# Two bottleneck blocks on one core: tiles as runs of 392 pixels, one tile less in the Gram matrix, three rows of the last tile made early

## The chip, the core and the metric

One core of a Trainium2 chip runs the whole program. The metric is the time of one execution on the device in microseconds (us). The kernel before takes 1884.95 us, the median of three runs (1884.44 to 1885.69).

## What is computed

Two bottleneck blocks stand one behind the other. Input and output are 64 images of 1024 channels and 14×14 pixels in fp32, which makes 64·196 = 12544 pixels in all. One block of the reference, cut to what matters:

```python
out = relu(_bn(_conv(x, w1, b1, 1, 0), g1, be1))      # 1x1, 1024 -> 256
out = relu(_bn(_conv(out, w2, b2, 1, 1), g2, be2))    # 3x3,  256 -> 256
out = _bn(_conv(out, w3, b3, 1, 0), g3, be3)          # 1x1,  256 -> 1024
out = softplus(residual_scale)[0] * out
return relu(x + out)
```

`_bn` takes mean and variance over images and pixels. So the sums over all 12544 pixels of a convolution's result have to be known before the first of its values can be normalized.

## The kernel before

Everything of 256 channels (`y`) stays in SBUF as `y_all`, 128 partitions by two slots `s` by 12544 pixels. The 12544 pixels are cut into 32 tiles `t` of 392 pixels (two images). In `y_all` a group of 8 images lies row by row, 112 pixels to a row, so a tile of two images is 14 runs of 28 pixels; `two(t, s)` (L88) gives that view. Values of 1024 channels are 8 rows `o` of 128 channels ("output rows"), and `x_t` is a tile of them, 128 partitions by 8·392.

The change bears on the end of block two, from about 1500 us on. It goes in three stages.

**The Gram stage.** The mean and the mean square of the third convolution's result are not taken from that result, which is not made yet, but from `y`: the Gram matrix of `y`'s 256 channels, with a column of ones, and the weights give both. `gram` (L1321) walks over the pixels by blocks of 128 pixels, two at a time (`CH`), 98 blocks or 49 pairs. A block has to stand with its pixels on the partitions; VectorE (DVE) transposes it by `turn` (L1310) from a buffer `home`, into which DMAs and ScalarE (ACT) have moved a piece of `y`. Then TensorE (PE) makes four products per block (`gram_products`, L1292) that add up in the banks `ap`. The pieces are listed in `moved`, and the last piece is the first 1536 pixels. At the start of the stage, while no block is there yet, PE convolves the first `HELD` = 5 rows of tile 0, and ACT copies them to `z` some time later.

**The gap.** When the last block is in, `conv3_stats` (L1745) makes the sums `mv` from the Gram matrix by a chain of small DVE and PE steps, and `affine` (L2031) makes `scale` and `shift`. PE has little to do meanwhile; rows 5, 6 and 7 of tile 0 (`conv3`, L1240) are put there.

**The last stage.** `final` (L1849) walks over tiles 1 to 30 by pairs t = 1, 3, …, 29 and by q = 0 to 3 in each pair; one (t, q) is a unit of class `Conv3Pair`, which makes rows q and q + 4 of both tiles by seven products instead of eight. A product goes to a PSUM bank `cx`, `cy` or `cp`; DVE adds it to a row of `x` (L533), or ACT copies it to `cu` (L336), from where GpSimd (POOL) adds it (L556, L664). Then ACT applies shift and relu (also L336), DVE does the same for one row in four (L673), and SP's queue sends the rows out (L676). Two units overlap. In the rows below, x_29 and x_30 are the last pair. The rows of tile 0 are finished beside the first units. Behind the last unit `ending` (L1823) makes tile 31 plainly: per row four PE records (two matmuls, a slot each, in two passes), the residual on DVE (`residual`, L1802, the instruction at L1807), the relu on ACT, and a DMA per two rows (L1840), the last ones smaller.

Each engine works through its instructions in the order that the code is recorded in; the recorder fixes the order when the program is built. An instruction that waits holds back all that stands behind it on its engine.

## Time and profile before

| what | value |
|---|---|
| median of three runs | 1884.95 us |
| the profiled execution's own time | 1884.47 us |
| its span, first to last instruction | 1882.7 us |
| PE busy | 1867.1 us, 99% |
| DVE busy | 1573.0 us, 84% |
| ACT busy | 1105.0 us, 59% |
| POOL busy | 742.5 us, 39% |
| bytes moved by DMA | 459.17 MB, 244 GB/s in the mean |

The span is 1.8 us shorter than the execution's time. PE's granted clock is full all along. In rows of a timeline the first number is the start in us, the second the time in us, and what stands in brackets is how long the engine sat idle just before and which engine and line ended that. "PEld" is the loading of weights, which overlaps PE, and SPq is SP's queue. A busy time printed for a group of matmuls includes the overlap of one with the next, so the starts say better than the lengths how fast PE goes.

### The profile page before, as it was taken

What the parts mean: (1) busy time and instruction counts of PE and PEld (TensorE: products, weight loads), DVE (VectorE), ACT (ScalarE), POOL (GpSimd) and SP (SyncE); (2) the same over time, 40 slices, a digit from 0 to 9 for tenths busy, and PEclk for the clock granted to TensorE, in tenths of its full rate; (3) what the DMA queues carried; (4) which work ended last, traced back from release to release, by engine and by line L of the source; (5) the groups of instructions that cost most, each with busy time, mean ns of one, the idle gap of its engine ahead of it and who ended that gap; (6) DMA issues with size and microseconds to landing.
All of it is one profiled execution on the core that took longest, in us unless ns stands there. A gap on an engine that the chain in (4) does not pass through costs nothing. (4 is left out here: it accounts for less than half of the span.)

```text
span 1882.7 us, 28588 instructions
## 1 busy us (share of the span) xinstructions
PE 1867.1 (99%) x9752; PEld 1559.0 (83%) x9752; DVE 1573.0 (84%) x2496; ACT 1105.0 (59%) x2301; POOL 742.5 (39%) x762
## 2 busy tenths in 40 slices
PE   9999999999999999999999999999999999999999
PEld 5555557999997998899999999999999987555555
DVE  5787867999998776778878888799999987888886
ACT  2222214677777665555555555457777794666666
POOL 0111100121205656377677776301121051666665
PEclk9999999999999999999999999999999999999999
DMA  7777654798765556678788789559788466999997
GB/s 289 269 253 270 216 188 128 211 215 220 206 197 169 186 173 212 248 272 312 275 287 307 276 307 278 209 169 220 213 208 227 135 179 245 350 336 333 349 338 280
DMA packets 263329, 459.17 MB, mean 244 GB/s; under 512 B 59376, under 2 KB 229712, under 8 KB 250000
## 3 DMA queue, kind: packets, MB, share of 16 engines
q1 hardware_dynamic: 224928, 375.47, 59.7%
q0 software_dynamic: 31408, 29.30, 8.0%
q10 hardware_dynamic: 6848, 52.57, 6.9%
q8 instruction: 77, 1.26, 0.3%
q14 instruction: 68, 0.56, 0.1%
HBM read 289.44 MB, written 141.03 MB: 229 GB/s over the span
## 5 line engine op out<-in xcount | busy, mean ns | idle before, releaser
L161 PE MATMUL columns<-v,ub 128*128 128x224 f32 (+1 forms) x1536 | 302.9, 339 | 1.3 <-ACT columns L336 0.8
L336 ACT ACTIVATE x<-x,shift 128x392 f32<-128x392 f32 x453 | 260.4, 613 | 70.4 <-DVE x L533 31.4
L161 PEld LDWEIGHTS columns<-v,ub 128*128 128x128 f32 x1536 | 268.6, 188 | 7.8 <-ACT columns L336 1.5
L336 ACT ACTIVATE cu<-cy,scale 128x196 f32<-128x196 f32 (+1 forms) x360 | 175.6, 500 | 166.6 <-PE cy L161 156.6
L161 PE MATMUL ay<-at,ws 128*128 128x196 f32 (+1 forms) x760 | 191.5, 383 | 0.4 <-ACT au L336 0.2
L664 POOL TENSOR_TENSOR x<-x,cu 128x392 f32<-128x392 f32 x120 | 126.0, 1051 | 104.9 <-DVE x L533 103.6
L161 PEld LDWEIGHTS ay<-at,ws 128*128 128x128 f32 x760 | 135.0, 190 | 35.5 <-ACT au L336 0.5
L533 DVE SCALAR_TENSOR_TENSOR x<-cp,scale,x 128x196 f32<-128x196 f32 (+1 forms) x240 | 124.7, 519 | 45.4 <-PE cp L161 43.9
L336 ACT ACTIVATE au<-ay 128x196 f32<-128x196 f32 (+1 forms) x139 | 53.5, 385 | 169.6 <-PE ay L161 159.6
L161 PE MATMUL l<-diffs,ub 128*128 128x224 f32 (+1 forms) x768 | 149.7, 337 | 0.5 <-DVE diffs L802 0.3
L161 PE MATMUL m<-sums,ua 128*128 128x224 f32 (+1 forms) x752 | 146.0, 337 | 1.2 <-issue 0.6
L161 PEld LDWEIGHTS l<-diffs,ub 128*128 128x128 f32 x768 | 134.6, 190 | 1.7 <-DVE diffs L802 0.7
L161 PEld LDWEIGHTS m<-sums,ua 128*128 128x128 f32 x752 | 131.4, 189 | 2.6 <-issue 1.0
L1103 POOL DMA_DIRECT2D y<-f x24 | 32.1, 1636 | 257.0 <-DVE f L1002 257.0
L161 PE MATMUL cx<-y,w 128*128 128x196 f32 (+1 forms) x400 | 123.1, 394 | 0.0
L556 POOL TENSOR_TENSOR x<-x,cu 128x196 f32<-128x196 f32 (+1 forms) x120 | 104.5, 871 | 45.8 <-ACT cu L336 28.7
L161 PE MATMUL cy<-y,w 128*128 128x196 f32 (+1 forms) x376 | 116.9, 399 | 1.8 <-ACT y L336 0.9
L336 ACT ACTIVATE y<-y,shift,scale 128x320 f32<-128x320 f32 (+9 forms) x107 | 110.7, 1061 | 7.1 <-DVE shift L2075 6.4
L561 POOL TENSOR_TENSOR x<-x,cu 128x392 f32<-128x392 f32 x60 | 80.3, 1339 | 85.1 <-DVE x L533 82.2
L208 POOL DMA_DIRECT2D u<-y x48 | 26.0, 543 | 211.1 <-ACT y L336 210.4
L1924 POOL TENSOR_SCALAR y<-y,scale 128x392 f32<-128x392 f32 x57 | 92.3, 1620 | 28.5 <-DVE scale L2268 28.5
L962 ACT ACTIVATE columns<-m 128x448 f32<-128x448 f32 (+1 forms) x144 | 70.9, 492 | 55.4 <-PE m L161 48.5
(315 smaller groups left out, 4508.2 us busy)
## 6 DMA issues: line engine op xcount, KB each, us to landing
ub<-u SPq DMA_DIRECT2D x92, 768.0 KB, 5.6
x<-in_x SPq DMA_DIRECT2D x35, 1568.0 KB, 8.5
x<-mid SPq DMA_DIRECT2D x32, 1568.0 KB, 7.7
out<-x SPq DMA_DIRECT2D x123, 392.0 KB, 6.7
mid<-x ACTq DMA_DIRECT2D x30, 1568.0 KB, 9.2
x<-in_x SPq DMA_DIRECT2D x108, 392.0 KB, 7.7
ua<-u SPq DMA_DIRECT2D x92, 256.0 KB, 3.2
z<-kept SPq DMA_DIRECT2D x60, 392.0 KB, 2.9
```

Source lines behind the costliest of these rows:

```text
L161: tc.keep_in_program_order(nc.tensor.matmul(*args, **kw))
L208: nc.gpsimd.dma_start(out=us[b][i][:, s, o], in_=u)
L336: tc.keep_in_program_order(nc.scalar.activation(*args, **kw))
L533: run(nc.vector.scalar_tensor_tensor(v, bank, self.scale[:, o : o + 1], v, ALU.mult, ALU.add))
L556: run(nc.gpsimd.tensor_add(self.part(1, 1), self.part(1, 1), u3))
L561: run(nc.gpsimd.tensor_add(v, v, self.u12))
L664: nc.gpsimd.tensor_add(v, v, self.u12[:, i * self.n : (i + 1) * self.n])
L962: copy(v, m, AF.Copy)
L1103: nc.gpsimd.dma_start(out=out_rows[3][:, o], in_=fa[:, o, :full], accum_op=ALU.add)
L1924: run(nc.gpsimd.tensor_scalar(z, z, scale[:, o : o + 1], None, ALU.mult))
```

## The change

Four things are changed.

1. `two(t, s)` is one run of 392 pixels (three and a half rows of 112 pixels of a group of images) and no longer 14 runs of 28. The host orders `x` and the result accordingly. All views with `h l` in them go.
2. Tile 0 is left out of the Gram matrix: the last piece of `moved` is (384, 1536) and no longer (0, 1536), `GRAM_TILES` is 48, and of the 98 blocks 95 remain, the last pair with one block alone. The 8 pixels of tile 0 that the piece still has are set to zero by a POOL memset (`leave_out`). Tile 0's part of the sums comes from its own eight rows: `save(o)` copies a row to `z` on ACT with a running sum (`accum_out`) and squares it in place with another, which gives `own`; DVE scales `own`, and `conv3_stats` adds it where it copied before.
3. For this, rows 5, 6 and 7 of tile 0 are convolved inside the last Gram piece and no longer in the gap.
4. The gap gets rows 0, 1 and 2 (`ENDED` = 3) of tile 31 in their place. ACT copies them to `held`. Their residual and relu are done in `final`, one beside each of the first three units of the last pair, and `ending` convolves rows 3 to 7 only.

The diff, cut to these:

```diff
+ENDED = 3
+GRAM_TILES = -(-(NPX - PX // P * P) // (CH * P))
...
     def two(t, s):
-        j = t % (GI // G)
-        return y_grp[:, s, t // (GI // G), :, j * G * W : (j + 1) * G * W]
+        return y_all[:, s, t * PX : (t + 1) * PX]
...
-        turned, moved = pieces[0], [*pieces[1:], (0, begin)]
+        whole = PX // P * P
+        turned, moved = pieces[0], [*pieces[1:], (whole, begin)]
...
+        def leave_out(k):
+            x, a, run = home(k)
+            nc.gpsimd.memset(x[:32, :, :, : PX - a], 0.0)
+
+        def save(o):
+            act(z[:, o], made[o], AF.Identity, accum_out=own[:, 0, o : o + 1])
+            act(made[o], made[o], AF.Square, accum_out=own[:, 1, o : o + 1])
...
-                    if k == len(moved) - 2 and i < len(made):
-                        act(z[:, i], made[i], AF.Copy)
+                    if k == len(moved) - 2 and i < HELD:
+                        save(i)
+                    if k == len(moved) - 1 and i < CS - HELD:
+                        o = HELD + i
+                        made.append(conv3(psum, 0, o, w3, ("cx", "cy")[i % 2]))
+                        save(o)
+            nc.vector.tensor_scalar(own, own, 1.0 / NPX, None, ALU.mult)
...
-        nc.vector.tensor_copy(mv[:, :, 0], sums[0][:, :, 0])
-        nc.vector.tensor_copy(mv[:, :, 1], sums[1][:, :, 0])
+        for i, ps in enumerate(sums):
+            if own is None:
+                nc.vector.tensor_copy(mv[:, :, i], ps[:, :, 0])
+            else:
+                nc.vector.tensor_add(mv[:, :, i], ps[:, :, 0], own[:, i])
...
+                if o >= ENDED:
+                    ps = psum.tile(PX // parts)
+                    for s in range(MS):
+                        matmul(ps, w3[:, s, o, :], two(T - 1, s)[:, here], start=s == 0, stop=s == MS - 1)
+                    residual(xt, o, ps, aff, here)()
...
                     while len(units) > 2:
                         units.pop(0).go_out()
+                    if t == T - 3 and q < ENDED:
+                        residual(xs[T - 1], q, held[:, q], aff)()
...
-                        made = [*(z[:, o] for o in range(HELD)), conv3(psum, 0, HELD, w3, "cx")]
+                        made = [conv3(psum, T - 1, 0, w3, "cx")]
+                        act(held[:, 0], made[0], AF.Copy)
...
-                    made += [conv3(psum, 0, HELD + 1 + i, w3, tag) for i, tag in enumerate(("cx", "ax"))]
+                    made += [conv3(psum, T - 1, 1 + i, w3, tag) for i, tag in enumerate(("cx", "ax"))]
                 aff = affine(mv3, pb, G3, BE3, conv_bias=B3)
+                if b == 1:
+                    for o in range(1, ENDED):
+                        act(held[:, o], made[o], AF.Copy)
```

Since the changed file is longer, some lines have new numbers after it: the matmul is L167 (before L161), ACT's helper L342 (L336), the residual L1816 (L1807), DVE's sums L536 (L533) and L676 (L673).

Three places show how the instructions move; the numbers behind the names are those of buffers. The first is PE's order at the end of the Gram stage. `ap<-zt` are the four products of a block, in three lines of which the first stands for two, and `cx<-y,w` and `cy<-y,w` are a plain row of the third convolution. After the change, from the second block of a pair on, with four and a half pairs of blocks still to come behind the first convolution:

```order
L167 MATMUL ap<-zt_11486 64x193 x2
L167 MATMUL ap<-zt_11486 64x129
L167 MATMUL ap<-zt_11486 64x130
L167 MATMUL cx<-y,w_1_11445 128x392 x2
L167 MATMUL ap<-zt_11487 64x193 x2
L167 MATMUL ap<-zt_11487 64x129
L167 MATMUL ap<-zt_11487 64x130
L167 MATMUL ap<-zt_11487 64x193 x2
L167 MATMUL ap<-zt_11487 64x129
L167 MATMUL ap<-zt_11487 64x130
L167 MATMUL cy<-y,w_1_11445 128x392 x2
```

Before, no convolution stands between the blocks: lines of `ap<-zt` follow one another up to the gap. Now rows 5 (`cx`), 6 (`cy`, the last line shown) and 7 (`cx`, one pair of blocks later) of tile 0 stand there.

The second place is DVE's order in the last pair. `x_29<-cx` and the like add a bank to a row of the pair. After the change:

```order
L536 SCALAR_TENSOR_TENSOR x_30_13851<-cp,scale,x_30_13851 128x392
L676 TENSOR_SCALAR x_27_13725<-x_27_13725,shift 128x392
L536 SCALAR_TENSOR_TENSOR x_30_13851<-cp,scale,x_30_13851 128x392
L536 SCALAR_TENSOR_TENSOR x_29_13849<-cy,scale,x_29_13849 128x392
L1816 SCALAR_TENSOR_TENSOR x_31_13973<-held,scale,x_31_13973 128x392 x3
L536 SCALAR_TENSOR_TENSOR x_29_13849<-cx,scale,x_29_13849 128x392
L536 SCALAR_TENSOR_TENSOR x_30_13851<-cp,scale,x_30_13851 128x392
L676 TENSOR_SCALAR x_27_13725<-x_27_13725,shift 128x392
```

Before, `x_29<-cy` and the `x_29<-cx` that is shown below it follow one another. Now the three residuals of tile 31 stand between them, all three in one place, where the pair's first two units overlap.

The third place is ACT's order there. `cu<-cy` copies a bank, and `x<-x,shift` is a relu. Before the change:

```order
L336 ACTIVATE x_28_13717<-x_28_13717,shift 128x392
L336 ACTIVATE x_27_13715<-x_27_13715,shift 128x392
L336 ACTIVATE x_28_13717<-x_28_13717,shift 128x392
L336 ACTIVATE cu_14051<-cy,scale 128x392
L336 ACTIVATE cu_14057<-cy,scale 128x392 x2
L336 ACTIVATE x_30_13841<-x_30_13841,shift 128x392
L336 ACTIVATE x_29_13839<-x_29_13839,shift 128x392
L336 ACTIVATE x_30_13841<-x_30_13841,shift 128x392
```

And after it:

```order
L342 ACTIVATE x_28_13727<-x_28_13727,shift 128x392
L342 ACTIVATE x_27_13725<-x_27_13725,shift 128x392
L342 ACTIVATE x_28_13727<-x_28_13727,shift 128x392
L342 ACTIVATE cu_14061<-cy,scale 128x392
L342 ACTIVATE x_31_13973<-x_31_13973,shift 128x392
L342 ACTIVATE cu_14069<-cy,scale 128x392 x2
L342 ACTIVATE x_30_13851<-x_30_13851,shift 128x392
L342 ACTIVATE x_29_13849<-x_29_13849,shift 128x392
L342 ACTIVATE x_30_13851<-x_30_13851,shift 128x392
```

The first relu of tile 31 stands between two copies: behind the last copy of unit q = 0 and ahead of the two copies of unit q = 1. The second and the third stand at the same place one and two units later.

More of the change, by code (lines that the diff above doesn't have):

```diff
@@ L1445, in pairs @@
             for k, (a, e) in enumerate(moved):
-                for i in range((e - a) // px):
-                    yield by_vector(k, i)
+                blocks = (e - a) // P
+                for i in range(-(-blocks // CH)):
+                    yield by_vector(k, i * CH, min(CH, blocks - i * CH))
                     if k + 2 < len(moved) and i in (1, 3):
@@ L1461, in gram @@
             if before is not None:
-                for c in range(CH):
-                    first, last = k == 1 and c == 0, k == total and c == CH - 1
+                n = before.shape[1]
+                for c in range(n):
+                    first, last = k == 1 and c == 0, k == total and c == n - 1
                     gram_products(upper, lower, before[:, c], first, last)
@@ L1565, in blocks @@
         def blocks(t):
-            return [[two(t, s)[:, i * H // 2 : (i + 1) * H // 2] for i in range(2)] for s in range(MS)]
+            return [[half_of(t, s, i) for i in range(2)] for s in range(MS)]
         n = PX // 2
```

100 lines of the change are left out of this document (42 added, 58 removed).

## The prediction

> **What bounds the kernel now.** I read the page's busy times first, then PE's waits, then the chain of waits from the Gram stage on, and last the timeline of the three places that the change touches.
>
> ```profile
> PE 1867.1 (99%) x9752; PEld 1559.0 (83%) x9752; DVE 1573.0 (84%) x2496; ACT 1105.0 (59%) x2301; POOL 742.5 (39%) x762
> ```
>
> PE is busy for 1867.1 of 1882.7 us: nothing but PE work taken away, or a new wait of PE's, moves the time much before the last few microseconds. The waits that PE has in the last stage are small:
>
> ```profile
> PE cy L161 <- ACT cu L336: 0.8, 4, 0.2
> ```
>
> All four waits for ACT's copies come to 0.8 us. So ACT's copies are in time now, and an edit that holds one back by more than its slack shows at once. The chain of waits has these rows at the end of the Gram stage:
>
> ```profile
> 1533.81 39.94 PE ap L161 x576
> 1573.75 1.51 PE cx L161 x4
> ```
>
> PE makes block after block without a pause: 576 records, at eight records a block (four products in two passes) 72 blocks, in 39.94 us, which is 0.555 us per block.
>
> **The change, part by part.**
>
> *Blocks left out.* Three of 98 blocks go, and PE is the limit there: 3 · 0.555 = **−1.66 us**. The zeroed pixels are one POOL memset, before the piece is transposed and on an engine that is idle there.
>
> *Rows moved.* The chain's rows of the ending:
>
> ```profile
> 1869.75 1.32 PE cx L161 x4
> 1871.06 1.32 PE cy L161 x4
> ...
> 1879.01 0.43 DVE x L1807
> ...
> 1879.47 0.46 ACT x L336
> ```
>
> A plain row costs PE 1871.06 − 1869.75 = 1.31 to 1.32 us. Three leave the ending (−3.95) and three more stand in the Gram stage (+3.95), where PE is the limit as well; the gap holds three rows as before, of another tile. On PE this is 0 in sum. The last stage starts 3.95 − 1.66 = 2.29 us later and its end is to come 3.95 us sooner after it.
>
> *ACT's saves.* Each of the eight rows of tile 0 costs ACT a copy and a square instead of a copy for five of them.
>
> ```profile
> L336 ACT ACTIVATE z<-cx 128x392 f32<-128x392 f32 x2 | 1.0, 505 | 0.0
> ```
>
> That is about 2 · 0.51 = 1.0 us per row, which the running sums may lengthen; no row shows those, so I bound it by 1.0 (they are free) and 2.0 us (they double it). The cover is ACT's and DVE's idle time at the end of the stage:
>
> ```profile
> 1573.86 1.56 DVE L1752 TENSOR_TENSOR g<-ap,by 64x65 f32<-64x65 f32 x5 [5.31 <-PE ap L161]
> ...
> 1574.94 0.20 ACT L1763 ACTIVATE g<-g 64x1 f32<-64x1 f32 x1 [12.60 <-DVE g L1752]
> ```
>
> ACT stood idle for 12.6 us before the gap and DVE for 5.3. The five early saves lengthen ACT's work by some 2.6 us. Row 7 leaves PE with five blocks to come, 5 · 0.555 = 2.8 us, so its save ends in front of the gap. `own`'s scaling on DVE waits for it, and then an add takes the place of a copy of the same few columns. I count all this as 0. If the saves took 2 us a row, the last would end about a microsecond after the last block, and the chain in the gap, on which PE waits, would be late by that: 0 to 1 us, and I take 0 by the row of 505 ns.
>
> *The residuals of tile 31.* They leave the ending, where PE was the limit, and stand in the last pair between instructions on which PE depends. In the order of ACT, the relu of row 0 now precedes the copies of the second unit, and in DVE's order its residual stands behind `x_29<-cy`. The rows of before at that place:
>
> ```profile
> 1853.06 1.20 ACT L336 ACTIVATE cu<-cy,scale 128x392 f32<-128x392 f32 x2
> ...
> 1854.78 0.82 PE L161 MATMUL cy<-ct,ws 128*128 128x392 f32 x2
> 1854.99 0.63 DVE L533 SCALAR_TENSOR_TENSOR x<-cy,scale,x 128x392 f32<-128x392 f32 x1
> 1855.03 1.01 POOL L664 TENSOR_TENSOR x<-x,cu 128x392 f32<-128x392 f32 x1 [0.32 <-DVE x L533]
> ...
> 1855.64 0.59 ACT L336 ACTIVATE cu<-cy,scale 128x392 f32<-128x392 f32 x1 [1.39 <-PE cy L161]
> ```
>
> The two copies of 1853.06 are the last of unit 0 and the first of unit 1; the second frees the bank that PE's product at 1854.78 writes. It ended at 1854.26, half a microsecond ahead. Now the relu stands between the two, and waits for a residual that DVE cannot start before `x_29<-cy` is through, at about 1855.55. Then POOL's sum runs until 1856.04. What that does to a DVE instruction with two operands in SBUF, as the residual of `held` is, shows one pair earlier:
>
> ```profile
> 1845.82 1.02 POOL L664 TENSOR_TENSOR x<-x,cu 128x392 f32<-128x392 f32 x1 [0.32 <-DVE x L533]
> ...
> 1846.43 0.83 DVE L497 TENSOR_TENSOR ct<-ct,y 128x392 f32<-128x392 f32 x1
> ```
>
> L497 ended at 1847.26, which is 0.42 us after POOL's end. Alone, a residual from SBUF takes 2.77 / 5 = 0.55 us:
>
> ```profile
> 1588.57 2.77 DVE L1807 SCALAR_TENSOR_TENSOR x<-z,scale,x 128x392 f32<-128x392 f32 x5
> ```
>
> So the residual ends at 1856.04 + 0.42 = 1856.46, the relu takes 0.55, the copy 0.59, and PE's product starts at about 1857.65 instead of 1854.78: **+2.87 us**. If POOL did not hold DVE up, the residual would end at 1855.55 + 0.55 = 1856.10, and the wait would be 2.5. The Trainium skill ("SBUF — State Buffer", section "Who interferes with whom") says that only the port pair which VectorE and GpSimd share is contended, "and it's an exclusive lock"; by this the residual is to stand still until POOL is done, as the row of L497 does, and the sum holds the 0.37 us more. The second and third relu stand at the same place one and two units later. Their residuals directly follow the first on DVE, are long done, and cost ACT 0.55 us each where the copy had 0.5 us to spare: +0.05 each, **+0.1 us**. DVE's next sum, `x_29<-cx`, comes 1.3 us later, which the wait of 2.87 us covers. The bounds of this part are 0, if x_31's row is ready before it is due in a way that I don't see, and what the second rival says.
>
> *The tail.* With 3.95 us less PE work, the last writes have less time.
>
> ```profile
> 1871.00:1877.00 6.00, 6.00 (x20) 3.50 (x19) 3.73 (x7) 3.28 (x6) 0.00 (x0) 1.00 1.02 383
> 1871.00:1882.00 11.00, 7.97 (x29) 4.89 (x27) 5.20 (x10) 5.33 (x10) 0.00 (x0) 1.00 0.78 291
> ```
>
> From 1871 on the DMA engines' mean busy share is 1.02 at 383 GB/s: they are full. 11 us at 291 GB/s are 3.20 MB. Rows 0 and 1 of tile 31 (0.39 MB) now go earlier, so 2.81 MB are left, 7.3 us at 383 GB/s, through at 1878.3 on the clock of before. The last issue and its landing:
>
> ```profile
> L1840 ACTq DMA_DIRECT2D out<-x x1: 344/344/344, 1880.0 to 1880.0; - x1
> ...
> DMA to landing us min/median/max: 1.7/2.1/4.0
> ```
>
> 1880.0 + 1.7 = 1881.7 was the last landing; by PE's chain it would be 1881.7 − 3.95 = 1877.75. The bytes are through at 1878.3, and I add 0.4 us for completion, since before the writes of the last 98 KB took 1.7 us from issue, of which the bytes are 0.3 and the rest spreads over issue and completion. 1878.7 against 1877.75 is **+1.0 us**, bounds 0 (rows 0 and 1 and one pair's rows go out earlier than I think) and 1.5 (the whole backlog plus a landing of 2.1).
>
> *Contiguous runs.* Whether `y` is read by runs of 28 or by 392 in one piece, the rows of the last stage show no difference:
>
> ```profile
> L161 PE MATMUL cy<-ct,w 128*128 128x392 f32 x117 | 48.2, 493 | 0.0
> L161 PE MATMUL cx<-y,w 128*128 128x392 f32 x116 | 47.7, 493 | 0.0
> L161 PE MATMUL cy<-y,w 128*128 128x392 f32 x116 | 47.7, 492 | 0.0
> ```
>
> `ct` is contiguous and `y` strided: 493, 493, 492 ns. I take 0.
>
> **Sum.** −1.66 + 2.87 + 0.1 + 1.0 = +2.3 us. The profiled execution took 1884.47 us (a span of 1882.7 and 1.8 around it) and would take 1886.8; the median of the runs is 0.5 above it, so on the runs I predict **1887.2 us**. A difference of 0.2%, 3.8 us, is about what a measurement of this kernel can tell from no change.
>
> **Rivals.**
>
> *The wait isn't there.* If the first residual is done in time (a record that the recorder puts elsewhere in time than I read, or slack on ACT that I missed), the gain of the blocks stays, and the tail takes between 0 and 1.0 of it: 1884.95 − 1.66 = 1883.3 to 1884.3. For it speaks that ACT is busy for 59% only; against it, that an engine's order is fixed and DVE's `x_29<-cy` cannot run earlier than the product it reads. Chance 0.22.
>
> *Tile 31 comes late: slower.* The first residual needs x_31, which nobody needed before the ending.
>
> ```profile
> L111 SPq DMA_DIRECT2D x<-mid x1: 325/325/325, 1847.1 to 1847.1; - x1
> ...
> DMA to landing us min/median/max: 7.7/7.7/7.7
> ```
>
> It was issued at 1847.1 and landed 7.7 us later, at 1854.8, only 1.2 us before POOL lets DVE go (1856.04). The loads of this pool from 1780 us on spread further:
>
> ```profile
> DMA to landing us min/median/max: 6.9/7.7/11.5
> ```
>
> With 11.5 us it lands at 1858.6, the residual ends at 1859.15 and not 1856.46, and everything behind is 2.7 us later still: +5.0, **1889.9 us**. The point from which it counts is a landing of 8.9 us; from 10.4 us on the whole is slower by more than 0.2%. For it speaks that the load shares the DMA engines with pair 27's writes; against it, that the change adds no transfer there and that 7.7 is also the median. Chance 0.16, of which 0.12 lies beyond 10.4 us.
>
> *Contiguous reads are faster.* The page has two groups of matmuls that read `y` as it lies:
>
> ```profile
> L161 PE MATMUL cx<-y,w 128*128 128x196 f32 (+1 forms) x400 | 123.1, 394 | 0.0
> ...
> L161 PE MATMUL cy<-y,w 128*128 128x196 f32 (+1 forms) x376 | 116.9, 399 | 1.8 <-ACT y L336 0.9
> ```
>
> These are 776 records; 8 ns off each would be 6.2 us and the time 1884.95 + 2.3 − 6.2 = 1881.0. The three rows above speak against it, with 1 ns between them. The Trainium skill ("Advanced Engine Details and Errata", section "PSUM Cachelines") has the rule that "Any non-contiguous AP significantly slows down matmuls"; the trace does not agree as far as it bears on the operand that is read, with 493 and 493 ns. Chance 0.05.
>
> **Chances.** Forecast 0.50, no wait 0.22, late tile 0.16, faster matmuls 0.05, and 0.07 for what I have not seen, of either sign. Forecast and first rival both lie within 0.2%. That makes 0.07 for faster, 0.77 for the same and 0.16 for slower. The range goes from the first rival's lower end to the second one's time: 1883.2 to 1890.0; the forecast's own terms (wait 2.5 to 2.9, tail 0 to 1.5, saves 0 to 1) reach from 1885.9 to 1888.7.
>
> **What would show it.** In the changed kernel's profile: the products `ap` end 1.66 us sooner but for three rows of 1.32 us among them; the gap keeps its length (if not, the saves are to blame); matmuls that read `y` stay at 492 to 494 ns; PE waits once for ACT's copy in the last pair, for 2.5 to 2.9 us, and ACT before it for DVE's residual (no such wait: first rival; a DVE wait for x_31's load: second); and the DMA engines are full from the last unit to the end, with a last landing about 2.7 us after the last matmul's relu. The forecast is wrong if PE's busy time falls by more than 2 us, or if the wait lies elsewhere.

## The result, and the profile after

The changed kernel takes 1890.66 us, the median of nine runs (1890.16 to 1891.72), against 1884.97 us for the kernel before on the same chip (nine runs, 1884.44 to 1886.55): a ratio of 1.0028, interval 1.0019 to 1.0037. It is slower by 5.7 us where +2.3 had been forecast, and lies just outside the range. The profiled execution took 1890.67 us with a span of 1888.9, which is 6.2 us more than before.

PE's busy time on the page of the changed kernel hardly differs from 1867.1:

```profile
PE 1867.8 (99%) x9728; PEld 1555.5 (82%) x9728; DVE 1573.1 (83%) x2494; ACT 1111.2 (59%) x2329; POOL 742.1 (39%) x763
```

So the time is in waits and in places where PE starts less often while it counts as busy. PE's waits in the changed kernel:

```profile
PE cy L167 <- ACT cu L342: 3.6, 5, 2.7
...
PE ap L167 <- DVE zt L1309: 0.9, 2, 0.6
```

The wait of 2.7 us is the one that the forecast named. The second row is PE waiting for DVE's transposes in the Gram stage, 0.2 us before. By PE's starts the 6.2 us divide as follows (us, from the timelines of the two profiled executions):

| stretch | before | after | difference | forecast |
|---|---|---|---|---|
| start of the first Gram product | 1518.14 | 1519.29 | +1.15 | 0 |
| Gram stage, first product to the row in the gap | 55.55 | 59.48 | +3.93 | +2.29 |
| gap, that row to the second row in it | 10.74 | 10.66 | −0.08 | 0 |
| the 120 records of PE from there on (first units of the last stage) | 40.87 | 41.57 | +0.70 | 0 |
| wait in the last pair | – | 2.87 | +2.87 | +2.97 |
| three rows of the ending | 3.95 | – | −3.95 | −3.95 |
| end of the last relu to end of span | 2.77 | 4.30 | +1.53 | +1.0 |

The first line lies ahead of all that runs differently; over the 14 profiles of this study (one execution each) that start lies between 1518.14 and 1520.00, and before is the earliest of them, so I count it as scatter.

**The Gram stage.** PE's rows of the changed kernel, from the long run of blocks to the gap:

```profile
1529.46 32.03 PE L167 MATMUL ap<-zt 128*64 128x193 f32 x464 [0.32 <-DVE zt L1309]
...
1562.11 6.80 PE L167 MATMUL ap<-zt 128*64 128x193 f32 x96 [0.62 <-DVE zt L1309]
...
1568.84 1.58 PE L167 MATMUL cx<-y,w 128*128 128x392 f32 x4
...
1570.36 1.32 PE L167 MATMUL ap<-zt 128*64 128x193 f32 x16
...
1571.60 1.58 PE L167 MATMUL cy<-y,w 128*128 128x392 f32 x4
...
1573.12 1.32 PE L167 MATMUL ap<-zt 128*64 128x193 f32 x16
...
1574.37 1.58 PE L167 MATMUL cx<-y,w 128*128 128x392 f32 x4
...
1575.88 2.96 PE L167 MATMUL ap<-zt 128*64 128x193 f32 x40
...
1578.78 1.58 PE L167 MATMUL cx<-y,w 128*128 128x392 f32 x4
```

The 39.94 us without a pause are broken by two waits for transposes, 0.32 + 0.62 = 0.94 us. A row among the blocks takes 1570.36 − 1568.84 = 1.52 us (then 1.52 and 1.51), not 1.32 as in the ending, and the pair of blocks behind it 1571.60 − 1570.36 = 1.24 us, where two blocks take 1.11. So each inserted row costs 0.20 us more in the row itself and 0.13 in the blocks behind it, some 0.33 us for going over from one kind of product to the other and back.

DVE is what PE waits for. The windows of the last full 15 us of transposing (PE, PEld, DVE, ACT, POOL busy, then clock and DMA), of the kernel before:

```profile
1550.00:1565.00 15.00, 15.00 (x220) 14.39 (x218) 15.00 (x29) 12.12 (x18) 5.50 (x10) 1.00 0.74 217
```

and of the changed kernel:

```profile
1550.00:1565.00 15.00, 14.38 (x210) 13.88 (x208) 14.74 (x26) 14.74 (x31) 6.79 (x19) 1.00 0.66 174
```

Before, PE *and* DVE were busy for 15.00 of 15 us. The forecast took PE for the one limit and made nothing of DVE's column here. DVE's rows say more about the two waits:

```profile
1528.70 1.30 DVE L1309 STREAM_TRANSPOSE zt<-home 128x512 f32<-128x512 f32 x2 [1.56 <-ACT y L342]
...
1552.69 1.30 DVE L1309 STREAM_TRANSPOSE zt<-home 128x512 f32<-128x512 f32 x2 [0.26 <-DVE zt L1309]
...
1561.36 1.29 DVE L1309 STREAM_TRANSPOSE zt<-home 128x512 f32<-128x512 f32 x2
```

Ahead of the first wait DVE itself had stood idle for 1.56 us, until ACT had a piece of `y` ready. From 1552.69 on DVE has no pause up to the transposes at 1561.36, for which PE waits the second time: there DVE's own work sets the pace. The 96 records behind that wait are the twelve blocks of the piece before the last, so neither the memset of the left-out pixels nor the landing of the last piece can have caused it.

**The saves**, on ACT in the changed kernel:

```profile
1570.46 0.50 ACT L342 ACTIVATE z<-cx 128x392 f32<-128x392 f32 x1 [5.03 <-PE cx L167]
1570.86 0.20 ACT L342 ACTIVATION_READ_ACCUMULATOR z<-cx 128x1 f32 x1
1570.95 0.49 ACT L342 ACTIVATE cx<-cx 128x392 f32<-128x392 f32 x1
1571.36 0.19 ACT L342 ACTIVATION_READ_ACCUMULATOR cx<-cx 128x1 f32 x1
```

Each running sum is an instruction of its own of 0.2 us. A row takes 1571.55 − 1570.46 = 1.09 us, and the last is done at 1577.08, 1.7 us before the gap: they cost nothing, as the gap's length says too.

**The last pair**, by all engines in the changed kernel:

```profile
1860.69 1.01 POOL L667 TENSOR_TENSOR x<-x,cu 128x392 f32<-128x392 f32 x1 [0.32 <-DVE x L536]
1861.18 2.02 DVE L1816 SCALAR_TENSOR_TENSOR x<-held,scale,x 128x392 f32<-128x392 f32 x3
1862.16 0.62 ACT L342 ACTIVATE x<-x,shift 128x392 f32<-128x392 f32 x1 [2.88 <-DVE x L1816]
1862.68 0.57 ACT L342 ACTIVATE cu<-cy,scale 128x392 f32<-128x392 f32 x1
...
1863.31 0.93 PE L167 MATMUL cy<-ct,ws 128*128 128x392 f32 x2 [2.71 <-ACT cu L342]
```

The residual waits behind POOL, the relu behind the residual (ACT idle for 2.88 us), the copy behind the relu, and PE's product behind the copy.

**The tail**, by windows of the changed kernel (columns as above):

```profile
1880.00:1884.00 4.00, 3.65 (x16) 2.37 (x14) 2.85 (x6) 2.75 (x5) 0.00 (x0) 1.00 1.02 373
1884.00:1888.00 4.00, 0.00 (x0) 0.00 (x0) 0.11 (x1) 0.46 (x1) 0.00 (x0) 0.73 0.80 292
```

The DMA engines are full at 1.02 while the last rows are made, and PE is done more than three microseconds before they are. In windows of 1 us from 1884 on they move 379, 394, 340, 53 and 0 GB/s: full almost to 1887, and then nothing for most of the last 1.9 us of the span.

**The first units of the last stage** hold 0.70 us that I had not looked at. Before, DVE's sum of two SBUF operands beside POOL's two sums:

```profile
1602.64 2.40 POOL L664 TENSOR_TENSOR x<-x,cu 128x392 f32<-128x392 f32 x2
...
1603.59 0.57 DVE L497 TENSOR_TENSOR ct<-ct,y 128x392 f32<-128x392 f32 x1
```

and the same three instructions in the changed kernel:

```profile
1607.65 1.98 POOL L667 TENSOR_TENSOR x<-x,cu 128x392 f32<-128x392 f32 x2
...
1608.61 1.45 DVE L502 TENSOR_TENSOR ct<-ct,y 128x392 f32<-128x392 f32 x1
```

DVE comes just as POOL goes from its first sum to its second. Before, DVE took 0.57 us, and POOL's two sums took 2.40; now POOL's take 1.98, and DVE takes 1.45. The Trainium skill ("SBUF — State Buffer", section "Who interferes with whom") has this as an exclusive lock that goes to whoever issues first, the other standing still; the lengths in the two traces agree, with 0.57 against 1.45 us. Who comes first cannot be read from the starts: in all 14 profiles DVE's is recorded 0.02 us ahead of POOL's second sum. In four of them (before, e1, e2, e5) DVE's instruction takes 0.57 us and PE's 120 records take 40.85 to 40.88; in the other ten it takes 1.45 and they take 41.56 to 41.63. As e2 and e5 have the change in them, this is not a cost of the change as such.

### The profile page after: what moved, and what is told of

Its sections match the earlier page's. It is cut to its first block, busy times and chain, and to the rows that moved or that the text cites. A ratio compares the mean times of both kernels' runs of the same rounds, so it can differ in the third digit from the quotient of the medians.

```text
span 1888.9 us, 28626 instructions
## 1 busy us (share of the span) xinstructions
PE 1867.8 (99%) x9728; PEld 1555.5 (82%) x9728; DVE 1573.1 (83%) x2494; ACT 1111.2 (59%) x2329; POOL 742.1 (39%) x763
## 5 line engine op out<-in xcount | busy, mean ns | idle before, releaser
L167 PE MATMUL columns<-v,ub 128*128 128x224 f32 (+1 forms) x1536 | 303.5, 339 | 1.4 <-ACT columns L342 0.8
L342 ACT ACTIVATE x<-x,shift 128x392 f32<-128x392 f32 x453 | 260.3, 613 | 71.7 <-DVE x L536 31.4
L167 PEld LDWEIGHTS columns<-v,ub 128*128 128x128 f32 x1536 | 268.6, 188 | 8.4 <-ACT columns L342 1.5
L342 ACT ACTIVATE cu<-cy,scale 128x196 f32<-128x196 f32 (+1 forms) x360 | 175.5, 499 | 163.0 <-PE cy L167 155.5
L167 PE MATMUL ay<-at,ws 128*128 128x196 f32 (+1 forms) x760 | 191.6, 383 | 0.4 <-ACT au L342 0.2
L167 PEld LDWEIGHTS ay<-at,ws 128*128 128x128 f32 x760 | 134.8, 190 | 35.7 <-issue 0.9
L536 DVE SCALAR_TENSOR_TENSOR x<-cp,scale,x 128x196 f32<-128x196 f32 (+1 forms) x240 | 124.4, 518 | 45.6 <-PE cp L167 44.2
L342 ACT ACTIVATE au<-ay 128x196 f32<-128x196 f32 (+1 forms) x139 | 53.5, 385 | 169.8 <-PE ay L167 159.8
L167 PE MATMUL l<-diffs,ub 128*128 128x224 f32 (+1 forms) x768 | 149.7, 337 | 0.4 <-DVE diffs L803 0.3
L167 PE MATMUL m<-sums,ua 128*128 128x224 f32 (+1 forms) x752 | 146.0, 336 | 1.2 <-issue 0.6
L167 PEld LDWEIGHTS l<-diffs,ub 128*128 128x128 f32 x768 | 134.6, 189 | 1.8 <-DVE diffs L803 1.1
L167 PEld LDWEIGHTS m<-sums,ua 128*128 128x128 f32 x752 | 131.4, 189 | 2.7 <-issue 0.9
L167 PE MATMUL cx<-y,w 128*128 128x196 f32 (+1 forms) x404 | 124.7, 395 | 0.0
L167 PE MATMUL cy<-y,w 128*128 128x196 f32 (+1 forms) x372 | 115.6, 398 | 1.7 <-ACT y L342 0.9
L342 ACT ACTIVATE y<-y,shift,scale 128x320 f32<-128x320 f32 (+9 forms) x105 | 110.2, 1074 | 7.1 <-DVE shift L2082 6.4
```

The source lines that it names most:

```text
L167: tc.keep_in_program_order(nc.tensor.matmul(*args, **kw))
L342: tc.keep_in_program_order(nc.scalar.activation(*args, **kw))
L536: run(nc.vector.scalar_tensor_tensor(v, bank, self.scale[:, o : o + 1], v, ALU.mult, ALU.add))
```

## The experiments

Theory after this first reading: the Gram stage costs more than forecast because of going over between blocks and rows (1.0 us) and because DVE, not PE, sets the pace at its end; the last pair's wait is ACT's order; the tail is bound by bytes. Rivals: the tiles cost something themselves; the order of DVE's side work, not its amount, makes the waits; the wait has another cause than the relu; the tail is latency. Names of lines below are those of each run's own kernel, which an edit shifts a little. The medians beside the ratios were measured on several chips, on which the kernel before takes 1884.98 to 1885.62 us.

**e1: the tiles alone** (parts 2 to 4 of the change undone, part 1 kept).

```diff
-        turned, moved = pieces[0], [*pieces[1:], (whole, begin)]
+        turned, moved = pieces[0], [*pieces[1:], (0, begin)]
...
-        total = GRAM_TILES
+        total = NPX // (CH * P)
```

> The kernel before with the contiguous tiles alone: the Gram matrix takes all 98 blocks, the gap holds rows 5 to 7 of tile 0, the ending makes all eight rows. Between the two profiled executions PE is already 1.2 us late at 1500 us, and another 0.65 us is lost at the start of the last stage. Theory: both are the scatter from one execution to another, and contiguous tiles cost nothing: within 0.5 us of before (1884.5 to 1885.5). Rival: the contiguous tiles cost them: 1.2 to 1.9 us above before, 1886.2 to 1886.9.

Measured: 1885.24 us (1884.56 to 1887.03) against 1885.17, ratio 1.0000 (0.9991 to 1.0009). Gram stage 55.91, first units 40.85, tail 2.77. Runs of 392 pixels cost and gain nothing that shows (the interval is 1.7 us to either side); the loss is in parts 2 to 4, and the rival of faster contiguous reads has fallen.

**e2: the relus of tile 31's rows one unit later**, their residuals in fixed places of DVE's order, the write of rows 0 and 1 ahead of the last unit. The relu of row 2 is left out by this edit.

```diff
-                    if t == T - 3 and q < ENDED:
-                        residual(xs[T - 1], q, held[:, q], aff)()
+                    if t == T - 3:
+                        if later:
+                            later.pop(0)()
+                        if q < ENDED:
...
+                            later.append(partial(act, v, v, AF.Relu, bias=aff[1][:, q : q + 1]))
```

> The changed kernel with the three relus of tile 31 one unit later each, their residuals in fixed places of DVE's order behind the sum that frees a bank, and the write of rows 0 and 1 behind the third. Theory of the held-up queue: PE's wait of 2.7 us for ACT's copy in the last pair goes, up to 0.4 us of another may come since two residuals still stand ahead of a sum on DVE: 2.4 to 2.9 us below the changed kernel. Rival: the wait moves to DVE's sums, which the residuals and the late load of x_31 hold up: less than 1 us gained.

Measured: 1889.61 us (1888.35 to 1890.75), ratio 1.0022 (1.0013 to 1.0031). PE's wait in the last pair:

```profile
1864.90 0.93 PE L167 MATMUL cy<-ct,ws 128*128 128x392 f32 x2 [0.47 <-ACT cu L342]
```

2.71 became 0.47, as the theory said; the edit moves the residuals too, so that the relu alone is not shown to be the cause here (e10 takes it out altogether). The last relu ended at 1881.59, 3.0 us sooner than in the changed kernel, but the span (1887.1) ended only 1.8 sooner: the tail grew from 4.3 to 5.5, so 1.2 of the 3.0 us went into the writes. The median is 1.1 us below the changed kernel's and not 2.4 to 2.9.

**e3: rows 5, 6 and 7 in one place** instead of three.

```diff
-                    if k == len(moved) - 1 and i < CS - HELD:
-                        o = HELD + i
-                        made.append(conv3(psum, 0, o, w3, ("cx", "cy")[i % 2]))
-                        save(o)
+                    if k == len(moved) - 1 and i == 0:
+                        for o in range(HELD, CS):
+                            made.append(conv3(psum, 0, o, w3, ("cx", "cy")[(o - HELD) % 2]))
+                        for o in range(HELD, CS):
+                            save(o)
```

> The changed kernel with rows 5, 6 and 7 of tile 0 convolved one after the other in one place of the last Gram piece, not in three. Theory: each change from the 64-column products to a 128-column row and back costs PE 0.33 us (0.2 going in, 0.13 coming back), so two changes less save 0.65 us, and in the profile the second and third row take 1.32 us instead of 1.52. Rival: the 0.2 us are a wait for the bank or for ACT that the profile does not name; then each row takes 1.52 us here as well, and the time is that of the changed kernel.

PE's rows there:

```profile
1569.30 1.58 PE L167 MATMUL cx<-y,w 128*128 128x392 f32 x4
...
1570.72 1.48 PE L167 MATMUL cy<-y,w 128*128 128x392 f32 x4
...
1572.04 1.48 PE L167 MATMUL cx<-y,w 128*128 128x392 f32 x4
...
1573.45 5.16 PE L167 MATMUL ap<-zt 128*64 128x193 f32 x72
...
1578.54 1.58 PE L167 MATMUL cx<-y,w 128*128 128x392 f32 x4
```

From the first row to the gap it is 1578.54 − 1569.30 = 9.24 us where the changed kernel has 1578.78 − 1568.84 = 9.94 for the same three rows and nine blocks: 0.70 less, two thirds of the price of going over, as two of three places are gone. The second row takes 1.32 us and the third 1.41, so the 0.2 us are not a wait for a bank or for ACT. The median, 1890.60 (1889.16 to 1892.94, ratio 1.0029), does not show it. In this profile the clock was halved behind the wait in the last pair, and of the six runs the three slowest (1891.34 to 1892.94) have a mean clock of 0.998, the other three 0.999 to 1.000; windows of the profile (the number ahead of the last two is the granted clock):

```profile
1864.00:1867.00 3.00, 3.00 (x6) 1.42 (x6) 1.05 (x2) 2.12 (x4) 0.96 (x1) 0.50 0.10 35
```

**e4: the first unit of the last pair sent out one unit sooner.**

```diff
-                    while len(units) > 2:
+                    while len(units) > (1 if t == T - 3 and q else 2):
```

> The changed kernel, in which the first unit of the last pair is sent out (0.78 MB, and its relu on DVE) one unit sooner, while the DMA engines are idle. Theory: the end is bound by the bytes that are left when PE is done, and 0.78 MB less of them take 2.0 us off that; PE's chain then ends it, 1.0 to 1.5 us below the changed kernel. Rival: what is late at the end is the completion of the last small writes and not the backlog: no difference.

Measured: 1890.29 us (1888.86 to 1891.88), ratio 1.0026 (1.0017 to 1.0035). Its last relu

```profile
1884.02 0.46 ACT L342 ACTIVATE x<-x,shift 128x196 f32<-128x196 f32 x1 [0.15 <-DVE x L1816]
```

ended at 1884.48, and the span at 1887.7: a tail of 3.2 us instead of 4.3. So 1.1 us of the tail are bytes that could have gone earlier. In the median only 0.4 us of it is to be seen, less than the scatter of these runs and less than the 1.0 to 1.5 us of the theory. That the tail is bytes and not latency shows beside the other profiles: from the last relu to the end of the span, 2.77 us at 133 GB/s (before), 3.24 at 163 (e4), 4.29 at 218 (the changed kernel) and 5.39 at 248 (e11) are 0.37, 0.53, 0.94 and 1.34 MB. Each is about 1.8 us and 1 us more for every 0.37 to 0.38 MB still to be written.

**e5: rows 5, 6 and 7 of tile 0 not convolved at all.**

```diff
-                        made.append(conv3(psum, 0, o, w3, ("cx", "cy")[i % 2]))
+                        made.append(made[i])
```

> The changed kernel without the convolution of rows 5, 6 and 7 of tile 0 in the Gram stage (ACT saves other rows in their place, so these three rows of the output and the sums are not the reference's). Theory: PE is the limit there, and a row costs it 1.32 us, and 0.33 for going over from the 64-column products and back: the Gram stage ends 3 times 1.65 = 4.95 us sooner. Rival: DVE's transposes are the limit in that piece, the rows fill time in which PE would wait for zt, and less than 3 us goes.

PE's rows at the end of the Gram stage:

```profile
1562.93 6.80 PE L167 MATMUL ap<-zt 128*64 128x193 f32 x96 [1.20 <-DVE zt L1309]
...
1570.50 5.16 PE L167 MATMUL ap<-zt 128*64 128x193 f32 x72 [0.77 <-DVE zt L1309]
...
1575.58 1.58 PE L167 MATMUL cx<-y,w 128*128 128x392 f32 x4
```

With no rows PE waits 0.26 + 1.20 + 0.77 = 2.2 us for DVE's transposes, and the stage takes 56.09 us, as long as with all 98 blocks (55.55 and, in e1, 55.91). But the last of the three waits is of the edit's own making. In the changed kernel the scaling of `own` stands behind all transposes in DVE's order; here it stands ahead of the last five, and waits for ACT's saves:

```profile
1569.04 0.17 DVE L1462 TENSOR_SCALAR own<-own 128x16 f32<-128x16 f32 x1 [1.99 <-ACT cy L342]
1569.73 2.82 DVE L1309 STREAM_TRANSPOSE zt<-home 128x512 f32<-128x512 f32 x5 [0.52 <-DVE own L1462]
```

Without these 0.77 us the stage would take some 55.3 (my estimate): with three blocks less **and nothing in their place, it would have become shorter by 0.2 us and not by 1.66** (0.6 against e1), in this one execution. The three rows cost 59.48 − 56.09 = 3.4 us here, or 4.2 by that estimate, so neither the theory (4.95) nor the rival (under 3) came out. The wait of 1.20 lies ahead of the place where the rows stand, so they do not fill it; ahead of it DVE had stood idle for 1.23 us, until ACT had its piece ready (at 1553.57). (One execution: 1888.25 us.)

**e7: DVE's side work (`pair_sums` and `combine_w3`'s second half) one pair of blocks later**, to let two transposes go first.

```diff
-                        beside = {total - 14 + 2 * i: partial(next, summed) for i in range(4)}
-                        beside[total - 4] = lambda: first_sums.append(pair_sums(sums_pool, 1))
+                        beside = {total - 13 + 2 * i: partial(next, summed) for i in range(4)}
+                        beside[total - 3] = lambda: first_sums.append(pair_sums(sums_pool, 1))
```

> The changed kernel with DVE's work for the last stage (the sums ws and ct), which is due at fixed counts from the end of the Gram stage, one pair of blocks later. It was moved up by one pair when the stage got one pair shorter; DVE's order is as before the change again. Theory: PE's wait for a transpose at 1562 us (0.6 to 1.1 us in four profiles, absent before) came from this and goes: 0.5 to 1.0 us below the changed kernel. Rival: it comes from the memset of the left-out pixels and the landing of the last piece, on which the first transpose of that piece waits: no difference.

Measured: 1890.59 us (1889.79 to 1893.40), ratio 1.0026 (1.0017 to 1.0036). The waits stayed, the last of them at the piece before the last:

```profile
1562.73 6.90 PE L167 MATMUL ap<-zt 128*64 128x193 f32 x96 [0.55 <-DVE zt L1309]
```

0.37, 0.42 and 0.55 us, 1.34 in all. Here the theory is not borne out, but it is not refuted either. Ahead of the first two waits DVE itself stood idle, 1.61 us for ACT and 1.92 for a DMA into `home`. And e9 and e11, which have the same order of DVE's work, show no wait above 0.1 us at this last place, where the eight profiles with 95 blocks and the change's order show 0.62 to 1.20. So the order seems to help; it was not the only cause.

This profile has something else that the changed kernel's has not. In the last pair the load of x_31 came late, and DVE's residuals waited for it:

```profile
1862.76 1.70 DVE L1816 SCALAR_TENSOR_TENSOR x<-held,scale,x 128x392 f32<-128x392 f32 x3 [0.74 <-DMA x<-mid]
```

PE's wait there is 3.21 us and not 2.71.

**e13: less work for DVE** (the sums of the weights on POOL).

```diff
-                    made_c, summed = combine_w3(w3, sums_tile(one, 1)[:, 0])
+                    made_c, summed = combine_w3(w3, sums_tile(one, 1)[:, 0], nc.gpsimd)
```

> The changed kernel with the four weight sums ws, which DVE makes among the last transposes of the Gram stage (0.65 us each), made by POOL. In seven profiles of kernels with 95 blocks PE waits 0.6 to 1.4 us for transposes in this stage, 0 to 0.2 us with 98. Theory: DVE is as much the limit there as PE, its side work being the same while PE's shrank; with 2.6 us less on DVE the wait at the last piece (0.5 to 1.1 us) is gone. Rival: the landing of the last pieces' transfers and the memset behind them set it; then the wait stays, with DVE idle ahead of its first transpose of that piece.

```profile
1557.69 10.60 PE L167 MATMUL ap<-zt 128*64 128x193 f32 x152
...
1568.22 1.58 PE L167 MATMUL cx<-y,w 128*128 128x392 f32 x4
```

No wait is left at that place (0.28 us early in the stage), and the stage takes 58.81 us, 58.53 without the 0.28. Before took 55.55 with 0.21 of waiting; the sum for a PE that never waits is 55.34 − 1.66 + 3 · 1.65 = 58.63. So both parts of the Gram stage's excess are there: 1.0 us of going over, and 0.6 to 1.2 us of waiting for transposes in the six profiles that have the rows in three places and DVE's work as the change left it (59.34 to 60.07 in all). It is one profile, and e9 below has no wait with all of DVE's work in place. The median, 1889.80 (1888.80 to 1892.47, ratio 1.0027), lies 0.9 below the changed kernel's; its profile had the clock halved as well.

**e8: e2 and e4 together**, with all three relus: the edits of both, and behind the last unit

```diff
+        for relu in later:
+            relu()
         for unit in units:
             unit.go_out()
```

> The changed kernel with the relus of tile 31 one unit later and the first unit of the last pair sent out one unit sooner. Theory: the wait in the last pair and the backlog at the end hang together, because the transfers drain while PE waits; the later relus alone made the tail longer (5.5 us from the last relu to the end, 4.3 in the changed kernel, 2.8 before). With both the tail is 3.2 to 3.8 us and the time 3.0 to 3.8 us below the changed kernel. Rival: the two add nothing to each other and the time is that of the later relus alone, 1 to 2 us below.

Measured: 1889.38 us (1888.12 to 1890.87), ratio 1.0019 (1.0011 to 1.0028). A new wait came up. DVE's rows and PE's, in the last pair:

```profile
1863.10 1.14 DVE L676 TENSOR_SCALAR x<-x,shift 128x392 f32<-128x392 f32 x2
...
1864.16 1.90 DVE L1876 SCALAR_TENSOR_TENSOR x<-held,scale,x 128x392 f32<-128x392 f32 x2
...
1866.71 0.93 PE L167 MATMUL cy<-ct,ws 128*128 128x392 f32 x2 [1.56 <-ACT cu L342]
```

Sending a unit out sooner puts two of DVE's relus in front of the residuals, where e2 has one. Two residuals take 1.9 us beside POOL in both, but in e2 the first is through in 0.61 us and the second waits, while here the first takes 1.37: the copy is late again. The two cures disturb each other, the tail is 4.3 us and not 3.2 to 3.8, and the time is about that of the later relus alone, as the rival said.

**e10: residuals in the last pair, relus and writes of rows 0 to 2 in the ending.**

```diff
-                    if t == T - 3 and q < ENDED:
-                        residual(xs[T - 1], q, held[:, q], aff)()
...
+        for o in range(ENDED):
+            residual(xs[T - 1], o, held[:, o], aff)()
         ending(psum, xs[T - 1], a, aff)
```

> The changed kernel with the relus (and so the writes) of rows 0 to 2 of tile 31 in the ending; their residuals stay on DVE in the last pair. Nothing waits on ACT ahead of its copies any more. Theory: PE's wait of 2.7 us is gone with no other in its place, and the last relu comes 2.8 us sooner; but the DMA engines then have 3.2 MB from the last pair on instead of 2.8, so the tail grows from 4.3 to 5.5 or 6 us and the time is only 1.2 to 1.8 us below the changed kernel. Rival: the tail does not depend on the bytes and the whole 2.8 us come off.

Measured: 1888.71 us (1888.23 to 1890.01), ratio 1.0019 (1.0010 to 1.0027). The recorder put DVE's residuals into the last pair, where one of them costs PE half a microsecond:

```profile
1867.93 0.93 PE L167 MATMUL cp<-y,ws 128*128 128x392 f32 x2 [0.49 <-DVE x L536]
```

No wait for ACT is left, and the median is 2.0 us lower. The last relu ends at 1881.32, 3.3 us sooner than in the changed kernel, of which 1.1 is an earlier start of the Gram stage in this execution; the tail takes 1.0 back and is 5.3 us long. So taking the wait out was worth some 2 us of the result and not its 2.87, with half a microsecond of a new one.

**e9 and e11: all cures together.** e9 has the edits of e8, e3 and e7. e11 has those of e3, e4 and e7 and, in the place of `residual` in e10, instructions that the recorder leaves in the ending:

```diff
+            v = xs[T - 1][:, o]
+            tc.keep_in_program_order(
+                nc.vector.scalar_tensor_tensor(v, held[:, o], aff[0][:, o : o + 1], v, ALU.mult, ALU.add)
+            )
+            act(v, v, AF.Relu, bias=aff[1][:, o : o + 1])
```

> The same with the three rows of tile 0 in one place and DVE's side work one pair of blocks later: all four repairs. Theory: the parts add up, 3.4 and 0.65 and 0.7 us below the changed kernel, 1885.5 to 1886.3, which is still not faster than before, since of the 1.66 us for three blocks 0.33 stay for going over to a row and back and about 0.8 in the tail. Rival: a wait that the others hid comes out, and less than 3 us is gained.

> The changed kernel with all repairs: residuals and relus of rows 0 to 2 of tile 31 in the ending, the first unit of the last pair sent out one unit sooner, the three rows of tile 0 in one place, DVE's side work one pair of blocks later. Theory: no wait of PE's in the last pair, 0.65 us less in the Gram stage, a tail of 2.8 to 3.5 us: 4.5 to 5.7 us below the changed kernel, equal to the kernel before within 1 us, because the tail and the going over use up what three blocks save. Rival: the parts overlap and the time stays 2 us or more above before.

e9: 1888.22 us (1887.07 to 1889.48), ratio 1.0015 (1.0006 to 1.0023). Gram stage 58.02 us with no wait (58.63 − 0.70 = 57.93 by the sum), a wait of 1.6 in the last pair as in e8; 2.4 us below the changed kernel, under 3 as its rival said. e11: 1887.17 us (1886.09 to 1888.97), ratio 1.0010 (1.0001 to 1.0019): the fastest version with the change in it, and still 1.9 us slower than the kernel before; 3.5 us below the changed kernel, where 4.5 to 5.7 were expected, with a tail of 5.4 and not 2.8 to 3.5. Its Gram stage, with the same edits as e9's, takes 58.71 us with one wait of 0.28 in the view, so some 0.5 us there are in no wait that the view lists. In its profile no wait is left in the last pair, and its last relu ends at 1880.05, 0.1 us behind before's 1879.93; its span ends 2.7 us later. The windows of e11 say why:

```profile
1871.00:1875.00 4.00, 4.00 (x14) 2.22 (x13) 3.71 (x6) 2.05 (x5) 3.08 (x3) 1.00 0.00 0
1875.00:1879.00 4.00, 4.00 (x17) 2.69 (x15) 3.99 (x8) 3.86 (x8) 0.00 (x0) 1.00 1.01 365
1879.00:1883.00 4.00, 0.10 (x1) 0.00 (x0) 0.42 (x1) 1.05 (x3) 0.00 (x0) 0.93 1.03 385
1883.00:1885.00 2.00, 0.00 (x0) 0.00 (x0) 0.00 (x0) 0.00 (x0) 0.00 (x0) 0.50 0.31 106
```

From 1875 on 4 · 365 + 4 · 385 + 2 · 106 KB = 3.21 MB go out, which is what the last two units (eight rows of 0.2 MB) and all of tile 31 (eight more) hold, and in the four microseconds before that nothing goes out. The kernel before wrote its last 3.2 MB from 1871 on. Sooner compute has left the same bytes to be written later. To send rows 0 and 1 of tile 31 into that hole without touching ACT's and DVE's order in the last pair was not tried.

**e12: the changed kernel again.**

> The changed kernel once more, for a second profile beside the others on the same chip. Theory: the wait of 2.7 us in the last pair stands in every execution, and behind it the granted clock is halved for 3.4 us in some (two of four profiles with that wait and no other edit near it), which costs 1.3 to 1.6 us more: the runs scatter over 1890 to 1893 us. Rival: the halved clock belongs to the edited kernels; the runs stay within 1 us.

Measured: 1891.12 us (1889.86 to 1892.03), ratio 1.0029 (1.0018 to 1.0041); the wait is 2.71 again, and the clock was not halved behind it, although this execution is the slowest of the six (its Gram stage starts 0.7 us later than the changed kernel's first profile and takes 0.6 more). The six runs spread over 2.2 us, so the rival (within 1 us) fell; that the halved clock makes the spread is not shown by this profile. Its windows (columns as above):

```profile
1864.00:1867.00 3.00, 2.37 (x7) 1.44 (x8) 1.23 (x3) 1.98 (x5) 0.00 (x0) 1.00 0.61 209
```

## Why the prediction was wrong, step by step

- **Blocks left out, −1.66 us: right as PE's work, but the time fell only in part.** e9 and e13 agree with a stage shortened by three blocks of 0.555 us. But "PE is the limit there" was half the truth: DVE was as full, 15.00 of 15 us, and with less work for PE its transposes are late. e5 shows the stage hardly shorter with the blocks gone and nothing in their place.
- **"On PE this is 0 in sum" is the step that failed.** It took a row at the ending's 1.32 us. Between Gram blocks a row costs 1.65 (1.52, and 0.13 on the pair behind), +1.0 us for three; e3 gave back 0.70 of it by having one place instead of three. With +0.73 us more waiting for transposes (0.94 against 0.21) the stage came out 1.64 us worse than forecast. Less their waiting, e13 (58.53) and e9 (58.02) agree with the sum of PE's own work within 0.1 us; e11 lies 0.5 us above it.
- **ACT's saves, 0: right**, though the running sum does cost 0.2 us each; the gap kept its length. Where `own` stands in DVE's order matters, as e5 shows.
- **Wait in the last pair, 2.87 us: right** in place, chain and size (2.71 of idle, a step 2.87 longer than without). The lock between POOL and DVE held the first residual as argued (0.94 us instead of 0.61). e2 put the relu a unit later and e10 took it out, and the wait fell to 0.47 and to none for ACT. The later two relus cost nothing.
- **Tail, +1.0 us: right in mechanism, mis-sized.** It measured +1.53, at the end of the bounds. The bytes were counted well (4 · 315 + 5.5 · 282 KB = 2.81 MB from 1879 on in windows of the changed kernel), but not all of them go at 383 GB/s: it is 315 from 1879 to 1883, and 379 to 394 from 1884 to 1886. The backlog behind the last relu, 0.94 MB against 0.37, accounts for the 1.5 us at 0.38 MB per us.
- **Contiguous runs, 0: right** (e1, ratio 1.0000).
- **Not in the sum at all:** 0.70 us in the first units of the last stage, where one DVE instruction took 1.45 us beside POOL and not 0.57. All 14 profiles split by that instruction's length, but none set the order on purpose, so that the whole 0.70 us is due to it is argued and not shown, and so is what decides the order.
- **Rivals.** "No wait" fell with the 2.71 us. "Tile 31 comes late" is not what made this result, although the time is near its 1889.9: ACT and DVE waited for POOL, and no wait for x_31's load is in the trace. But the rival is no fiction: in one of the seven profiles with the residuals at this place (e7) DVE waited 0.74 us for that load, and PE 0.50 longer.

These make up 1.15 + 1.64 − 0.08 + 0.70 − 0.1 + 0.53 = 3.8 of the 3.9 us by which the profiled span missed the forecast. The 1.15 at its head is, as far as known, scatter between executions. Neither sign that the prediction names for being wrong came: PE's busy time did not fall, and the wait in the last pair lies where it said. What did not come is the first item of its list, that the products `ap` end 1.66 us sooner but for three rows of 1.32 us among them.

What stays open: how much of the waiting for transposes is DVE's own work and how much the pieces of `y` that come late from ACT and the DMAs (behind DVE's idle times of 1.5 to 2.0 us for them PE waits 0.3 to 0.6 in eight profiles), and what sets the order at the port that POOL and DVE share.

## What to carry to other kernels

Price work that is moved into a stage in that stage: look at the second-busiest engine there before calling the first the limit, and add what it costs to go over from one kind of product to another. Compute that ends sooner gains little once the last writes are bound by bytes; what counts then is when each row is ready to go. An instruction put ahead of a PSUM-freeing copy on an in-order engine costs its own wait, and curing that by moving work to the next engine can set up the same wait one unit later.

## What the runs showed of the hardware

A pause of PE can cost more than itself. Behind the long wait in the last pair (2.7 us, in e7 3.2), four of the seven profiles that have it (e3, e5, e7, e13) show a granted clock of 0.50 for 3.41 us, the starts of e3's records 0.65 us apart instead of 0.33, worth 1.5 to 1.7 us; the other three (the changed kernel, e4, e12) show 1.00. Behind waits up to 1.6 us (e2, e8, e9, e10) it was never seen. The Trainium skill ("TensorE: Matmul & The Clock Gate", section "HAM oscillation — how this bites in real kernels") sets the limit for PE's pauses at some 3.4 us; here 2.7 us were enough in four of seven.

The traces' own records of the clock show what decides. In each profile the granted clock changes only at whole multiples of 3.413 us, counted from where it first stood at full: after 550 of them (1877.33 us) in the kernel before, after 551 (1880.74) in the changed kernel, and after 544 (1856.85) where the halved stretch of e3, e7 and e13 begins. On this grid PE was idle for 2.80 (e7), 2.53 (e3), 2.44 (e13) and 2.17 us (e5) of the one interval ahead of the halved one. In the three profiles that stayed at full speed the pause lies across a boundary so that no interval has more than 1.94 (e4), 1.66 (e12) and 1.38 us (the changed kernel). The drop at the end of each execution fits as well: over 14 profiles each of the 18 drops follows an interval with 2.17 us or more of idleness, and none follows one with 1.94 or less. So a pause of 2.7 us halves the clock or not by where it falls on the grid, which differs from execution to execution; this goes with the wide scatter of the runs of e3 and e13, whose slowest (three of six, four of ten) are those with a mean clock of 0.998. The length of the interval agrees with the free-running window of 3413 ns that the Trainium skill gives ("TensorE: Matmul & The Clock Gate", section "What's actually happening").

The port that POOL and DVE share changes a time by steps, not smoothly: one DVE sum takes 0.57 or 1.45 us and nothing between in 14 profiles, with the same recorded distance to POOL's next sum to within 0.005 us.
